# Unused products in the foreseen gaps of TensorE, in a planned convolution and attention kernel

## The chip, the cores and the metric

The kernel runs on one core of a Trainium2 chip. The metric is the device time of one execution in microseconds. TensorE is written PE here, its weight loads PEld, VectorE DVE, ScalarE ACT, GpSimd POOL, and SyncE, which issues most DMAs, SP.

## The reference

The input is 32 images of 128 channels by 64 by 64, in float32, as is everything else. Cut to what matters:

```python
x = x + conv(_gn(x))                  # group norm; 3x3 kernel mixed per image from 4 by a gate
t = _to_tokens(x)                     # 4096 tokens of 128 channels per image
t = t + attn(_ln_t(t))                # 128 -> 16, windows of 144 with stride 72, 4 heads of 4,
                                      # back to 128, added to its input, layer norm
t = t + ffn(_ln_t(t))                 # W, batch norm over all tokens, then a recurrence:
#   y_t = sigmoid(wx_t + y_{t-1} @ V.T)
```

The gate is a softmax over the sigmoid of `pooled @ fc_w.T + fc_b`, with the mean of each channel of the normalised image. The batch norm needs the statistics of all images before the recurrence can start.

## The kernel before, in words

There are two stages. The first, in `images`, runs the convolution, the attention and the product with W for every image and writes the result to `z_d` in DRAM. The second, `by_runs`, is the recurrence; it cuts the 4096 steps into runs of 32 with 16 steps to warm up each and works on four streams at once. The change does not touch it.

In the first stage the work of an image is cut into jobs, each a Python generator that yields before every step and says which engine the step needs and which tiles it reads and writes: `load` (statistics, the gate, the mixed kernel `h`), `taps` and `waves` (the transformed kernels `w` and rows `u` of a fast convolution), `conv` (its products), `drain` (their sum back into `frames`), `project` (layer norm, down to 16 channels), `feed` (queries, keys and values), `values` and `attend` (scores into the tile `sc`, exponentials `ex`, weighted sums into `av`), `divide` (division by the sums, product with `wc` into `sc`, addition to `zt`), `tail` (a layer norm) and `last` (product with `fWc`, statistics). A further job, `setup`, makes constants once.

A planner runs all jobs side by side while the program is built. The class `Clock` keeps for each engine the time at which it is free, and for each tile when it was last written and read, from a table of costs[...]. In each turn the planner takes the job whose next step can start first. Where several can start at the same time, the smaller due time is taken: the image's number plus the first number in `DUE`, plus the second one spread over the job's steps:

```python
a, w, n = DUE.get(job[0], (-1.0, 0.0, 1))
key = at, job[1] + a + w * job[4] / n - (9 if len(job[3]) > 4 else 0)
```

So the order on each engine is the planner's, fixed in the built program[...]. What the planner expects and what the chip does can differ.

[...]`sc` takes four (a single tile for scores and for the divide's products), `nm0` to `nm2` are one bank each and are handed out from the list `nms` to all other products, and one bank is `av`. A step that needs a bank takes it out of `nms` and puts it back once its reader has been recorded. For a step of PE the planner adds 0.25 to the expected start (`SAFE`).

Inside `load`, the gate product is short but stands on a chain: the product `nm<-cv,grp`, then ten small steps of DVE and ACT for the inverse deviation `gr`, then `h<-dev,gr`, then the product with `fcwT`.

In the profile nearly all instructions of the first stage carry one line, L242, since the recording helper issues them; the tiles' names tell them apart. A float32 product appears as two records.

## Time and profile before

| | us |
|---|---|
| median of 3 runs | 4502.47 |
| lowest and highest of them | 4498.48, 4503.09 |
| the profiled execution, own time | 4507.87 |
| its span in the trace | 4506.1 |
| PE busy | 4099.9 |
| DVE busy | 3562.1 |
| ACT busy | 2407.2 |
| POOL busy | 1680.8 |

The mean granted clock of TensorE in the profiled execution is 0.958. The first stage ends near 3962 us, where the recurrence's loads of `z_d` begin; its last 200 us are the drain, in which no new image enters. In a line of the profile's groups, the columns are line, engine, operation, tile written and tiles read, shapes and count, then busy time in us and the mean of one in ns, then the engine's idle time ahead of them and what ended it. In the waits, they are who waited for whom, the total in us, the times and the longest.

### The profile page before, as it was taken

Reading aid. Unit: us, or ns where it says so; the run is one execution under the profiler, and the core shown is the slowest. Engines: PE = TensorE matmul, PEld = TensorE weight load, DVE = VectorE, ACT = ScalarE, POOL = GpSimd, SP = SyncE. Lnnn points to the kernel's source line nnn. Section 1 sums busy time; section 2 is a strip of 40 time slices with the busy share of each in tenths; the row PEclk is TensorE's granted clock in tenths of the full one; section 3 lists DMA queues with packets and bytes.
Section 4 is the critical chain, followed back from the end, with each engine's and each line's share of the span. In section 5 each row is a group of like instructions: output and inputs, shape, how many; then the busy total and the mean of one; then the engine's idle time right before and its main releaser. Section 6 shows DMA issues by size and latency. Waiting matters only on the chain. (4 is left out here: it accounts for less than half of the span.)

```text
span 4506.1 us, 101240 instructions
## 1 busy us (share of the span) xinstructions
PE 4099.9 (91%) x41515; PEld 2055.8 (46%) x41515; DVE 3562.1 (79%) x5364; ACT 2407.2 (53%) x3500; POOL 1680.8 (37%) x1652
## 2 busy tenths in 40 slices
PE   5999889999999999999999999999999997589987
PEld 2444444444444444444444444444444444245443
DVE  7787778888788888788888788888888864459884
ACT  1455545555555555554555555554555565357774
POOL 3443333333334333333334333333333422037665
PEclk9999999999999999999999999999999998789998
DMA  3445454554555555555555456455465544459998
GB/s 101 132 144 161 150 172 153 182 175 157 184 167 177 175 175 182 171 178 166 190 171 180 144 176 189 150 175 177 152 191 166 167 166 168 157 215 257 280 264 170
DMA packets 467567, 789.31 MB, mean 175 GB/s; under 512 B 338048, under 2 KB 348304, under 8 KB 434320
## 3 DMA queue, kind: packets, MB, share of 16 engines
q1 hardware_dynamic: 456480, 715.38, 48.5%
q0 software_dynamic: 8704, 67.11, 7.2%
q8 instruction: 331, 5.42, 0.5%
q14 instruction: 148, 1.21, 0.1%
q10 hardware_dynamic: 1904, 0.18, 0.0%
HBM read 499.06 MB, written 276.76 MB: 172 GB/s over the span
## 5 line engine op out<-in xcount | busy, mean ns | idle before, releaser
L242 ACT ACTIVATE ex<-sc 128x1728 f32<-128x1728 f32 x672 | 1082.5, 1611 | 869.0 <-PE sc L242 854.6
L242 POOL TENSOR_TENSOR qe<-qs,mqk 128x576 f32<-128x576 f32 x448 | 608.8, 1362 | 992.4 <-PE sc L242 990.0
L242 PE MATMUL nm<-u,w 128*128 128x512 f32 x1536 | 779.9, 625 | 24.8 <-POOL w L242 24.6
L242 PE MATMUL sc<-qe,ks 32*128 32x432 f32 (+1 forms) x7168 | 689.0, 455 | 83.9 <-DVE zt L242 39.2
L242 PE MATMUL av<-ex,VE 128*32 128x144 f32 x14336 | 634.2, 296 | 3.0 <-DVE avs L242 2.0
L242 PEld LDWEIGHTS av<-ex,VE 128*32 128x32 f32 x14336 | 396.5, 111 | 309.7 <-issue 250.8
L242 PEld LDWEIGHTS sc<-qe,ks 32*128 32x128 f32 x7168 | 294.0, 190 | 481.7 <-issue 182.2
L1960 PE MATMUL v<-yw,fVT 128*128 128x254 f32 (+1 forms) x1504 | 438.3, 430 | 36.4 <-ACT yw L1973 25.5
L242 POOL TENSOR_TENSOR u<-frames 128x528 f32<-128x528 f32 x256 | 411.1, 1614 | 60.1 <-PE nm L242 57.3
L1971 ACT ACTIVATE yw<-v,shf 128x254 f32<-128x254 f32 (+1 forms) x752 | 353.7, 473 | 123.9 <-DVE v L1966 48.3
L1966 DVE SCALAR_TENSOR_TENSOR v<-zr,scl,v 128x256 f32<-128x256 f32 (+1 forms) x585 | 347.1, 663 | 92.0 <-PE v L1960 91.9
L242 PEld LDWEIGHTS nm<-u,w 128*128 128x128 f32 x1536 | 262.9, 191 | 328.8 <-issue 288.6
L242 PE MATMUL nm<-u,h 128*128 128x512 f32 x768 | 391.1, 622 | 0.5 <-ACT tm L242 0.5
L242 ACT ACTIVATE place<-zt 128x1024 f32<-128x1024 f32 x256 | 261.4, 1052 | 208.1 <-DVE zt L242 180.2
L1960 PEld LDWEIGHTS v<-yw,fVT 128*128 128x128 f32 x1504 | 241.6, 194 | 246.0 <-ACT yw L1971 195.7
L242 POOL TENSOR_TENSOR kt<-ks,mqk 128x384 f32<-128x384 f32 (+1 forms) x96 | 79.4, 827 | 654.8 <-ACT ks L242 432.0
L1977 POOL COPY zr<-yw 128x256 f32<-128x256 f32 x416 | 257.2, 729 | 86.2 <-ACT yw L1971 85.8
L242 PE MATMUL nm<-zt,fWc 128*128 128x512 f32 x512 | 283.5, 649 | 6.3 <-ACT zt L242 6.3
L242 DVE SCALAR_TENSOR_TENSOR u<-u,u 128x528 f32<-128x528 f32 x256 | 247.6, 983 | 25.4 <-POOL u L242 22.8
L242 PE MATMUL nm<-place,avg 128*32 128x256 f32 x3072 | 239.8, 395 | 12.9 <-ACT place L242 12.8
L242 DVE COPY avs<-av 128x288 f32<-128x288 f32 x224 | 100.6, 449 | 190.7 <-PE av L242 189.6
L242 PE MATMUL sc<-avs,wc 17*128 17x288 f32 (+1 forms) x1536 | 174.8, 516 | 69.8 <-DVE zt L242 51.0
(203 smaller groups left out, 6121.3 us busy)
## 6 DMA issues: line engine op xcount, KB each, us to landing
place<-r_d SPq DMA_DIRECT2D x384, 512.0 KB
place<-in_conv_k_dram SPq DMA_DIRECT2D x128, 576.0 KB
x_d<-frames SPq DMA_DIRECT2D x32, 2112.0 KB
place<-x_d SPq DMA_DIRECT2D x128, 528.0 KB
frames<-in_x_dram SPq DMA_DIRECT2D x128, 512.0 KB
out_dram<-zt SPq DMA_DIRECT2D x64, 1024.0 KB
z_d<-zt SPq DMA_DIRECT2D x64, 1024.0 KB
zr<-z_d SPq DMA_DIRECT2D x26, 2048.0 KB
```

The source lines that it names most:

```text
L242: got = f(*args, **kw)
L1960: nc.tensor.matmul(self.ps[:, :, c], fVT, self.yw[1 - r % 2][:, :, c], start=not whole, stop=True)
L1966: nc.vector.scalar_tensor_tensor(v, z, scl, v, ALU.mult, ALU.add)
L1971: nc.scalar.activation(y[:, :, c], self.ps[:, :, c], AF.Sigmoid, bias=shf)
L1977: nc.gpsimd.tensor_copy(z, y)
```

## The change

A constant `SPARE` of three numbers is added, and seven lines in the planner. Whenever the planner has chosen a step of PE, after `setup` is done, it looks at the gap between the time at which PE is free and the step's expected start less 0.3. If that gap is over 0.6 and a bank of `nms` is free by then, it issues products of 128 by 128 by 128 (`fWc` with itself) into that bank until 60% of the gap is filled. Nothing reads them. They are recorded in the planner's `Clock` like any other product. Besides, five entries of `DUE` have other numbers: `setup`, `taps`, `project`, `tail` and `last` are moved and spread differently.

```diff
+SPARE = 0.3, 0.6, 0.6
 DUE = {
-    "setup": (0.27, 0.02, 8),
+    "setup": (0.44, 0.04, 8),
...
-    "taps": (-0.14, 0.29, 6),
+    "taps": (0.04, 0.16, 6),
...
-    "project": (0.55, 0.51, 33),
+    "project": (0.75, 0.37, 33),
...
-    "tail": (2.4, 0.8, 33),
-    "last": (3.05, 0.62, 40),
+    "tail": (2.42, 0.75, 33),
+    "last": (2.99, 0.86, 40),
 }
...
                 job = best[1]
+                if job[3][0] == "PE" and "setup" in done:
+                    at = best[0][0] - SPARE[0]
+                    ready = [t for t in nms if clock.after("PE", t, True) <= clock.free["PE"]]
+                    if ready and at - clock.free["PE"] > SPARE[1]:
+                        t, until = ready[0], clock.free["PE"] + SPARE[2] * (at - clock.free["PE"])
+                        while clock.free["PE"] < until:
+                            nc.tensor.matmul(t[:, 0:P], fWc, fWc, start=True, stop=True)
                 job[4] += 1
                 job[3] = next(job[2], "end")
```

## The prediction

> **What bounds the kernel now.** I read the busy shares and the slices of the page first, then a table of stages, then TensorE's waits, then two of these waits in the timeline.

> ```profile
> PE 4099.9 (91%) x41515; PEld 2055.8 (46%) x41515; DVE 3562.1 (79%) x5364; ACT 2407.2 (53%) x3500; POOL 1680.8 (37%) x1652
> ...
> PE   5999889999999999999999999999999997589987
> ...
> DVE  7787778888788888788888788888888864459884
> ...
> PEclk9999999999999999999999999999999998789998
> ```

> TensorE (PE) is the bound from 112 to 3750 us, VectorE (DVE) stands close behind at eight tenths, and the granted clock is slightly below full nearly everywhere. The stages (columns: PE, PEld, DVE, ACT, POOL busy, clock, DMA share, GB/s):

> ```profile
> 112.00:708.00 596.00, 555.76 (x6170) 275.57 (x6169) 466.98 (x691) 302.91 (x401) 214.20 (x179) 0.97 0.49 154
> ...
> 2126.00:3546.00 1420.00, 1348.12 (x14954) 666.16 (x14953) 1188.72 (x1717) 761.74 (x1020) 504.07 (x409) 0.97 0.54 173
> ...
> 3750.00:3965.00 215.00, 118.26 (x1313) 57.82 (x1306) 102.24 (x156) 80.10 (x104) 20.59 (x16) 0.77 0.45 155
> ```

> Adding up the trace's clock records: from 112 to 3750 us the clock is at half in 36 stretches, 201 us together, and PE is busy for 168.4 us of them. At full clock that work takes half as long, so at most 84 us are lost there. PE is idle for another 195 us of this stage. In the drain (3750 to 3965) 44 us of busy time run at half.

> What opens the gaps, of the waits of PE from 112 to 3750 us (total, times, longest):

> ```profile
> PE sc L242 <- DVE zt L242: 75.5, 39, 4.7
> PE nm L242 <- DVE h L242: 49.7, 19, 3.5
> PE sc L242 <- ACT ex L242: 19.9, 45, 1.2
> ```

> The first wait is the divide's product into the one `sc` tile, which VectorE has not emptied; the second is the gate product with `fcwT` in `load`; the third is the next scores waiting for the exponential. From 708 to 3546 us, 39 gaps of 1.6 us or more hold 106 of 143 us of idle time. The order repeats every three images (355 us), with two late gate products and one pair of divide products in each:

> ```profile
> 1675.17 0.35 PE L242 MATMUL nm<-fcwT,h 128*128 128x4 f32 x2 [2.96 <-DVE h L242]
> ...
> 1694.45 1.01 PE L242 MATMUL sc<-avs,wc 17*128 17x432 f32 x8 [2.49 <-DVE zt L242]
> ...
> 1699.30 0.86 PE L242 MATMUL sc<-qe,ks 32*128 32x144 f32 x8 [3.83 <-DVE zt L242]
> ```

> And the clock around that pair:

> ```profile
> 1693.10:1696.50 3.40, 1.01 (x8) 0.31 (x8) 3.33 (x5) 0.00 (x0) 0.00 (x0) 1.00 0.33 123
> 1696.50:1699.90 3.40, 0.60 (x8) 0.61 (x12) 3.37 (x7) 0.99 (x1) 0.00 (x0) 0.51 0.00 0
> 1699.90:1703.30 3.40, 3.40 (x48) 2.36 (x42) 3.33 (x5) 2.18 (x3) 1.25 (x2) 0.50 0.55 231
> ```

> A stretch with 1.01 us of work is followed by two at half clock. In all 36 cases the 3.4 us ahead hold at most 1.87 us of work.

> [...]

> **The change, part by part.** Compared instruction by instruction, the changed program has 607 unused 128x128 products in 145 groups; 56 groups have two, 30 three, 13 four, 30 five, the last one 72. No other product is added; the DUE values only reorder. The first product of 66 groups waits for the bank's reader (57 ScalarE, 9 VectorE), the others for nothing[...]. From the tenth image on the order again repeats every three images, with 42 unused products in twelve groups, against none.

> *Price of one.* The f32 products nm<-wvB,gt of the same shape are two records 0.112 us apart, so 0.22 us; three took 0.87 us to the next start with the switch, 0.29. I take 0.22: the groups are runs. 607 x 0.22 = 134 us (176 at 0.29), in gaps as far as there are gaps.

> *(a) The clock.* Of the 168.4 us at half, 39.6 follow the divide pair, 70.5 the gate product, 58.3 other waits; half of each is the loss: 20, 35, 29. In the new order no two divide products stand together without 0.86 us of work and five unused products between them: all 20 return. No group stands directly ahead of a gate product, but it is late less often (next part): half, 17.5. Of the others half, 14.5, since the groups stand ahead of products that wait for DVE. **52 us.** Bounds: 0 and 84.

> *(b) The order.* Between the product with cv and the gate product lie VectorE's and ScalarE's steps for gr. PE's own work in between was 3.9, 2.8 and 3.7 us in the three images, and is 2.2, 12.1 and 9.6. In the first of the new ones VectorE's order is like that of before's on-time case, whose chain took 4.1 to 4.2 us: 2.0 us late. In the second, VectorE's work (13 steps, at before's means) is about 12.1: on time. In the third 12.6 against 9.6: up to 3.0 late, I take 1.5. So 3.5 us per cycle, times 10.2 cycles in 3638 us: 36 us instead of 49.7, **14 saved**. The divide pair's 2.49 + 3.83 us (eight times, 50 us) become 2.49 - 0.86 = 1.6 per cycle, 16 us; but the work between scores and the next scores is thinner (0.8 to 1.3 us in seven places, where the next can start 1.73 to 1.82 us after, by before's waits), some 2 us more per cycle, 20 us: **14 saved**. Bounds of (b): 40 lost, 60 gained.

> *(c) Products that outlast their gap.* 18 of the 42 stand ahead of products into sc that can't start before 1.8 us after the last scores: 4.0 us of them in 4.8 us of waiting, but three groups are too long, 0.75 us together. The other 24 fill 60% of what was foreseen, and VectorE was later than foreseen where before shows it; I take a tenth of their 5.3 us. 1.3 us per cycle: **13 us lost**. Bounds: 0 and 134.

> *(d) Given back.* VectorE is busy for 0.83 of the cycle; a faster PE waits for it sooner. A third of (a) and (b): **27 lost**. Bounds: 0 and 60.

> *(e) The drain.* 22 us are lost to the clock there, and 190 unused products stand after the last convolution; PE mostly waits there for VectorE and DMAs, so a third: **7 gained**. Bounds -5 and 22. The recurrence after 3965 us (by_runs) has the same instructions: 0, give or take 5 for where its clock windows fall. The start, with setup and taps later: 0, give or take 8. SP's and POOL's queues get the same DMAs and operations, in another order; their time is in (b).

> Sum: 52 + 14 + 14 - 13 - 27 + 7 = 47 us. The profiled execution took 4507.87 us, so 4461; it stands 5.4 us above the median of the runs, 4502.47: **4455 us**.

> **The rivals.**
> - *Nothing is given back*, and the drain gains fully: 52 + 28 - 13 + 22 = 89, so 4413 us. For it: VectorE still has a sixth of its time free. Against: its waits fall in the same places.
> - *The groups stand where no window was lost.* Only the divide pair's windows return (20), the order brings nothing, 13 are lost to overlong groups and 7 given back: 4502 us, no change. For it: the late gate products get no group of their own. Against: the foreseen waits behind the exponential and the divide are real in before. That an unused product waits itself for its bank and so fills nothing is of this case.
> - *The foreseen gaps are not there* (slower). When PE runs behind the plan, what it waits for is ready, and each group is pure addition, ahead of the product that could start. At 70% of 134 us the loss is 94 instead of 13: 4455 + 81 = 4536 us. It decides from 60 us on, 45% of the products. For it: in before, gaps under 0.9 us hold only 33 us of 2838. Against: the 1.8 us after scores.

> **How the numbers follow.** Forecast 0.63 (4425 to 4490), nothing given back 0.12, no change 0.12, slower 0.13. The range leaves out about one in ten on each side: 4400 to 4522; both ends lie inside the summed bounds above. Faster by over 0.2% (9 us, about what a measurement here can tell): 0.80, with the fast part of the third case; within 0.2%: 0.06; slower: 0.14.

> **What would show it.** Right: half-clock stretches from 112 us to the drain fall from 36 to about 15, with busy time in them from 168 to 65 us; the wait for `h` is 30 to 40 us; nm<-fWc rows of about 1214 records appear, mean clock 0.97 to 0.98. (c) is wrong if sc rows start right at the end of a group where before had none of that wait; (d) if the wait of sc for zt stays under 40 us. The whole is wrong if the half-clock time stays above 160 us, or if PE's idle time falls by less than its busy time grows.

## The result, and the profile after

The changed kernel took 4455.53 us (median of 4 runs, 4448.11 to 4460.42) against 4500.48 us for the kernel before: a ratio of 0.9908, interval 0.9887 to 0.993. Timed again it gave 0.9894 (0.9878 to 0.991). The profiled execution took 4460.42 us and its span is 4458.6 us, against 4507.87 and 4506.1. The forecast was 4455 us.

Parts 1 and 2 of the page of the kernel after, the lines that answer to those of before:

```profile
PE 4180.4 (94%) x42729; PEld 2191.2 (49%) x42729; DVE 3554.4 (80%) x5364; ACT 2410.3 (54%) x3500; POOL 1691.4 (38%) x1652
...
PEclk9999999999999999999999999999999999899998
```

PE has 1214 records more, the 607 products, and is busy for 80 us longer, though the span is 47.5 us shorter. VectorE's work is unchanged. The stages of the kernel after (columns: PE, PEld, DVE, ACT, POOL busy, clock, DMA share, GB/s):

```profile
112.00:1066.00 954.00, 920.04 (x10157) 472.78 (x10156) 776.02 (x1124) 495.19 (x660) 344.80 (x280) 0.98 0.51 161
1066.00:3501.00 2435.00, 2373.78 (x26731) 1222.73 (x26730) 2059.41 (x2996) 1335.03 (x1781) 890.04 (x714) 0.99 0.55 176
...
3705.00:3915.00 210.00, 150.76 (x1592) 93.94 (x1592) 99.62 (x150) 74.56 (x95) 13.76 (x12) 0.84 0.44 153
3915.00:4458.60 543.60, 478.56 (x1620) 265.63 (x1620) 403.14 (x726) 366.66 (x769) 339.17 (x544) 0.94 0.88 239
```

The clock in the middle of the first stage went from 0.97 to 0.99, in the drain from 0.77 to 0.84. The recurrence is as long as it was (544.6 us before, counted from its first product, 543.3 after): all of the gain lies in the first stage. PE's waits after, who waited for whom, total, times, longest:

```profile
PE sc L243 <- DVE zt L243: 33.2, 47, 2.3
...
PE sc L243 <- POOL qe L243: 21.6, 9, 2.9
...
PE sc L243 <- ACT ex L243: 14.4, 54, 0.5
...
PE nm L243 <- DVE h L243: 9.8, 4, 3.8
```

The wait for `zt`, over the whole execution 90.2 us before, fell to 33.2, and the wait of the gate product for `h` from 52.6 to 9.8. New is a wait of the scores for GpSimd's `qe`, 21.6 us in place of 2.6. A wait counts here only from the end of the unused products that stand in it, so a smaller one need not mean that its product came earlier.

For a balance I cut the stretch from 112 us to the recurrence's first product into four terms. *Clock* is half of the time that PE is busy while the clock records say half: in before, the records of the product `nm<-u,w` (128x512) start 854 ns apart at half clock and 429 ns at full (medians of 13 and 1074 intervals). In before and after the clock records say 1 or 0.5 and, but for the last one of each, have lengths in multiples of 3.413 us; such a stretch is what the forecast calls a window. *Unused* is the number of unused products in the stretch times 0.22 us (at full clock their records, two to a product, start 112 ns apart in the kernel after). *Idle* is the time without a PE record. *Work* is what is left. All four are worked out from the one profiled execution of each kernel, in us; sums in the text are taken before rounding. The names other than before and changed are the experiments of the next section.

| kernel | stretch | work | unused | idle | clock |
|---|---|---|---|---|---|
| before | 3849.5 | 3454 | 0 | 291 | 105 |
| changed | 3803.3 | 3460 | 129 | 164 | 50 |
| change_again | 3807.5 | 3462 | 129 | 168 | 47 |
| planned_only | 3823.9 | 3444 | 0 | 298 | 82 |
| doubled | 3853.0 | 3446 | 259 | 117 | 31 |
| large_groups | 3807.7 | 3448 | 85 | 227 | 48 |
| small_groups | 3810.7 | 3457 | 44 | 244 | 65 |
| untold | 3842.9 | 3474 | 126 | 184 | 59 |
| gate_fill | 3840.4 | 3459 | 24 | 276 | 82 |
| measured_fill | 3815.3 | 3466 | 43 | 247 | 59 |
| queries_fill | 3803.1 | 3466 | 140 | 169 | 28 |
| due_only | 3909.0 | 3443 | 0 | 349 | 117 |
| spare_only | 3905.2 | 3463 | 148 | 222 | 73 |

From before to changed, idle and unused together stay the same (291 and 294 us): the gaps are as long as they were, and the unused products lie in them. What is gone is 55 us of half clock; work rose by 6. The balance compares single executions: between before and planned_only the stretch differs by 26 us, but the medians on one chip by 16, so differences of some 10 us in it are no finding.

### The profile page after: what moved, and what is told of

The parts are those of the page before. It is cut to its first block, busy times and chain, and to the rows that moved or that the text cites. A ratio compares the mean times of both kernels' runs of the same rounds, so it can differ in the third digit from the quotient of the medians.

```text
span 4458.6 us, 103741 instructions
## 1 busy us (share of the span) xinstructions
PE 4180.4 (94%) x42729; PEld 2191.2 (49%) x42729; DVE 3554.4 (80%) x5364; ACT 2410.3 (54%) x3500; POOL 1691.4 (38%) x1652
## 4 chain that ended last, share of the span: by engine, by line
PE 61%; DVE 20%; DMA 9%; issue 4%; ACT 2%; SPq 2%; POOL 1%; DVEq 0%; ACTq 0%; POOLq 0%
PE nm L243 33%; PE sc L243 13%; PE av L243 10%; DVE zt L243 6%; PE v L1968 3%; DVE v L1974 3%; DVE frames L243 2%; DMA zr<-z_d 2%; DVE cp L243 2%; SPq L243 2%; ACT ex L243 2%; DMA out_dram<-zr 2%; DVE h L243 1%; DVE st L243 1%; DMA place<-x_d 1%
## 5 line engine op out<-in xcount | busy, mean ns | idle before, releaser
L243 PE MATMUL sc<-qe,ks 32*128 32x432 f32 (+1 forms) x7168 | 669.6, 443 | 41.9 <-POOL qe L243 21.6
L243 PE MATMUL av<-ex,VE 128*32 128x144 f32 x14336 | 624.6, 292 | 5.7 <-DVE avs L243 5.4
L243 POOL TENSOR_TENSOR u<-frames 128x528 f32<-128x528 f32 x256 | 392.8, 1544 | 37.1 <-PE nm L243 34.5
L243 ACT ACTIVATE place<-zt 128x1024 f32<-128x1024 f32 x256 | 259.8, 1050 | 175.9 <-DVE zt L243 166.6
L243 DVE SCALAR_TENSOR_TENSOR zt<-sc,gbk,zt 128x576 f32<-128x576 f32 (+1 forms) x192 | 174.5, 909 | 70.0 <-PE sc L243 69.0
L243 DVE TENSOR_TENSOR zt<-frames,place 128x1024 f32<-128x1024 f32 x128 | 211.5, 1682 | 21.2 <-DMA place<-r_d 21.2
L243 ACT COPY zt<-nm 128x512 f32<-128x512 f32 x256 | 149.1, 584 | 141.0 <-PE nm L243 139.7
```

Source lines behind the costliest of these rows:

```text
L243: got = f(*args, **kw)
```

## The experiments

My theory was that the clock brings the gain, and that the order counts only in how it lays out the gaps. The rivals were that the new order saves waiting, and that VectorE takes back what a faster PE gains. All ratios are to the kernel before, run on the same chip as the kernel in question.

**The changed order without the products.** They are noted in the planner's clock, so that every engine has the changed order, and not issued:

```diff
-                            nc.tensor.matmul(t[:, 0:P], fWc, fWc, start=True, stop=True)
+                            clock.note("PE", "matmul", (t[:, 0:P], fWc, fWc), dict())
```

> The changed order on every engine, but the 607 unused products are only noted in the planner's clock and not issued. Theory (the products keep the clock, the order brings little): the half-clock stretches come back, PE busy in them from 100 to about 190 us between 112 us and the recurrence, so some 45 us lost: 4495 to 4505 us, like before. Rival (the new order brings the gain by its shorter waits, the products cost about what they bring): 4455 to 4475 us.

Measured: 4482.51 us, ratio 0.997 (0.9957 to 0.9982). Between the two expectations: the order alone brings 0.3%, the products on top of it some 0.7% (0.9908 and 0.9894 against 0.997). The balance suggests how the order does it: not by less waiting (298 us idle against 291), but by less half clock, 82 us against 105, and 10 us less work. The waits of PE in this run:

```profile
PE sc L243 <- DVE zt L243: 76.0, 50, 4.1
PE sc L243 <- ACT ex L243: 41.4, 75, 1.8
...
PE nm L243 <- DVE frames L243: 29.0, 25, 1.9
...
PE nm L243 <- DVE h L243: 9.8, 4, 3.8
```

With the order alone all but four of the gate product's late arrivals are gone; in their place there are more and shorter waits, for the exponential (28.2 us in before) and for `frames` (8.1 us in before). From 112 us to the drain 28 half-clock stretches are left of 36. That the shorter gaps are the reason is inferred from this; no run tests it by itself.

**The same products with one column.** After the notes, as many products as were noted are issued, with the same bank and the same waits, but one column:

```diff
+                        for _ in range(n):
+                            clock.nc.tensor.matmul(t[:, 0:1], fWc, fWc[:, 0:1], start=True, stop=True)
```

> The changed order, and every unused product is issued with one column instead of 128, with the same bank and the same waits. Theory[...]: as without the products, 4495 to 4507 us, with half-clock time as there. Rival (the early wait for the bank's reader, or merely something issued in the gap, brings the gain): 4455 to 4470 us.

Measured: 4489.95 us, ratio 0.9982 (0.9972 to 0.9992), and a mean clock of 0.961 against 0.963 without any product and 0.975 with the full ones. The group of these products and that of the full ones (columns: line, engine, operation, tiles, shapes and count; busy us, mean ns of one; idle ahead). With one column:

```profile
L1423 PE MATMUL nm<-fWc 128*128 128x1 f32 x1214 | 188.4, 277 | 0.8 <-DVE frames L243 0.8
```

In the kernel after, with 128:

```profile
L243 PE MATMUL nm<-fWc 128*128 128x128 f32 x1214 | 175.9, 291 | 0.4 <-DVE frames L243 0.4
```

In the profile both fill PE for about the same time, and both come with 1214 weight loads. Only with the full ones was the mean clock higher than without any product, 0.975 against 0.963. Of the other products, 150 us run at half clock here, 164 in planned_only and 88 in the changed kernel. So something merely issued in the gap, or an earlier wait for the bank, does not bring the gain. The one-column products are no gain over none at all (4489.95 us against 4482.51, with intervals that overlap).

**Before's order with products that the planner isn't told of.**

```diff
+                        f = clock.free["PE"]
+                        while f < until:
+                            clock.nc.tensor.matmul(t[:, 0:P], fWc, fWc, start=True, stop=True)
+                            f += 0.22
```

> The kernel before with its own due numbers and its own order; 592 unused products fill 60% of the gaps that its plan foresees, and the planner is not told of them. Theory (clock): the pair of divide products no longer lets the clock fall, the late gate products still do, as no plan foresees them; about 20 to 35 of the 84 us return and 10 are lost to overlong groups: 4475 to 4490 us. Rival (the order is what counts): no change, 4495 to 4510 us. Rival (products alone bring all): 4455 us.

Measured: 4503.74 us, ratio 1.0014 (1.0005 to 1.0023), slower than before by a hair and in the range of the rival that expected no change, though not for its reason: the clock's mean rose to 0.974, and its loss fell from 105 to 59 us. I had expected 10 us of cost; the balance shows 39: idle and unused together went from 291 to 310, and work rose by 20. So here a higher clock brought no time by itself. The gate product stayed late:

```profile
PE nm L245 <- DVE h L245: 53.1, 20, 3.4
```

**Twice as many products**, `range(2 * n)` with full columns.

> The changed order, with two unused products for each one of the change (1214, nominally 120% of the foreseen gaps). Theory (the gaps are real and mostly as long as foreseen or longer): a group outlasts its gap by some 20 to 40% of the gap's 0.22 us steps, so of the 134 us added 40 to 70 lie on the path, while the clock returns 5 to 10 us more: 4485 to 4520 us. Rival (the chip runs later than planned, the gaps have room): 4445 to 4465 us. Rival (the gaps are hardly there): over 4560 us.

Measured: 4510.34 us, ratio 1.003 (1.002 to 1.004). Of the 129 us added in the stretch, idle time took up 47, the clock returned 19 more, to a loss of 31, and work fell by 14; the other 50 us made the stretch longer: that unused products hold up the work behind them was the forecast's assumption, and here it is the nearest reading. The forecast range held. The gaps have some room left at 60% but not at 120%; nothing in between was run.

**Large groups only, small groups only**: `n if n > 3 else 0` (405 products in 59 groups), and `n if n <= 3 else 0` (202 in 86).

> The changed order; of the unused products only the 405 that stand in the 59 groups of four or more are issued, the 202 in groups of two or three are only noted. Theory (long gaps let the clock fall, short ones don't, and a short gap is filled or overrun at no use): the clock stays as with all groups, PE busy at half 95 to 115 us against 99, and the small groups' cost of up to 10 us goes: 4445 to 4460 us. Rival (all gaps count alike, so two thirds of the products bring two thirds of the gain between 4482 without products and 4455): 4464 us. Rival (the short ones alone hold windows just above the limit): 4470 us or more.

> The changed order; only the 202 products in the 86 groups of two or three are issued. Theory (long gaps count): the half-clock time stays that of the order without products, 150 to 170 us of busy time, and the small groups cost up to 10 us: 4480 to 4495 us. Rival (all count alike): 4473 us. Rival (the short ones count): 4455 to 4462 us.

Measured: 0.9901 (0.9883 to 0.9918) with the large ones, at 4462.66 us against 4505.16, and 0.9941 (0.9925 to 0.9958) with the small ones, at 4476.53 us. The large groups alone give what the change gives; the clock's loss is 48 us there and 50 with all groups. The saving of 10 us that I expected from dropping the small ones can't be seen: work is 12 us lower, but idle and unused together are 18 higher. The small ones alone stand 0.3% under the order without products (0.997), against my theory that short gaps count for nothing; 0.9941 is what the rival expected that counts all alike (4473 us of 4500). But the two intervals just touch, and the ratios come from two chips, so this is weakly shown. With both, the small ones add nothing that can be seen.

**Each half of the change with its own plan**: the new due numbers without SPARE, and SPARE with the old numbers.

> The five new due numbers without SPARE; the planner makes another order, in which the cycle of three images doesn't appear. Theory (the due numbers fit the plan with products in it and have no worth of their own): no faster than before, 4495 to 4540 us, as the order jumps between patterns. Rival (the due numbers bring the 0.3% that the changed order brought by itself): 4475 to 4490 us.

> SPARE and its seven lines with the due numbers of before; 693 products in 162 groups, told to the planner, which makes another order without a cycle of three images. Theory (the products keep the clock in any order, but overrun their gaps where the order is not in step): clock 0.97 or more, half-clock busy time 100 to 120 us, time 4480 to 4510 us. Rival (the products alone, told to the planner, bring the gain): 4450 to 4465 us.

Measured: due_only 4566.31 us, ratio 1.013 (1.011 to 1.0149); spare_only 4561.29 us, ratio 1.0123 (1.0105 to 1.0141). Both are slower than either expectation. The clock loss is 117 us in the first and 73 in the second; what costs the time is the gaps, 349 us idle in one and 370 idle and unused in the other against 291. Neither order falls into the cycle of three images. So neither half of the change is a gain by itself; the numbers suit the plan that has the products in it, and the 0.3% of planned_only belong to that plan.

**Products at the late gate product, in before's order.** Here the gap is known from the trace, not from the plan; `unused(t, n)` issues n of the products into bank t, and the planner isn't told:

```diff
+                if b >= 5 and b % 3 != 1:
+                    unused(lg_ps, 6)
                 nc.tensor.matmul(lg_ps[:, 0:NK], pl, fcwT, start=True, stop=True)
```

> The kernel before, its order and plan unchanged; six unused products (108 in all) stand directly ahead of each of the 18 gate products that came 2.2 to 3.0 us late in its trace. Theory (a stretch of 3.4 us with under 1.9 us of work costs the clock, and at an unchanged order half or more of the clock's gain reaches the end): PE busy at half falls by some 55 us, 27 us at full clock, of which VectorE lets half through: 4480 to 4490 us against 4500. Rival (VectorE's chain sets the pace there, a faster PE only waits longer): idle time grows by what the clock returns, 4495 to 4505 us. Rival (all comes back): 4473 us.

Measured: 4495.93 us, ratio 0.9966 (0.9953 to 0.9978). One of these places in its timeline (start, duration, what, idle time ahead):

```profile
1659.13 1.50 PE L461 MATMUL nm<-fWc 128*128 128x128 f32 x12
1661.69 0.39 PE L242 MATMUL nm<-fcwT,h 128*128 128x4 f32 x2 [1.05 <-DVE h L242]
```

The clock in stretches of 3.4 us around such a place in before, where the product came at 1675.17 us:

```profile
1672.70:1676.10 3.40, 0.93 (x8) 0.96 (x8) 3.02 (x9) 0.20 (x2) 1.99 (x2) 0.99 0.37 142
1676.10:1679.50 3.40, 3.40 (x34) 1.52 (x33) 1.22 (x5) 1.72 (x4) 0.00 (x0) 0.50 0.23 68
```

and around the place above:

```profile
1659.30:1662.70 3.40, 2.35 (x20) 2.11 (x19) 3.03 (x9) 0.65 (x2) 1.99 (x2) 1.00 0.62 184
1662.70:1666.10 3.40, 3.20 (x54) 2.06 (x56) 2.53 (x9) 2.70 (x8) 0.00 (x0) 1.00 0.15 44
```

The stretch with the wait now has 2.35 us of work in place of 0.93, the product comes when VectorE is ready, and the clock stays full. Of the 18 places, 16 had a half-clock stretch within 4 us in before, and one has here. That shows the cause of these stretches. The clock's loss fell by 23 us, less than the 27 expected, since new half-clock stretches came up elsewhere; 15 us (0.34% of 4509) reached the end. As a share of before, which took 4509.53 us on this chip, that lies in the range of the theory. The wait for `zt` grew:

```profile
PE sc L242 <- DVE zt L242: 99.8, 47, 4.7
```

It was 90.2 us in before, so some of the gain was given back in waiting for VectorE.

**Also at the divide pair**, 196 products in all.

```diff
+                        pair = d and b % 3 == 0 and 6 <= b < 30
+                        if pair and u and nms:
+                            unused(min(nms, key=lambda t: clock.after("PE", t, True)), 5)
...
+                        if pair and u and nms:
+                            unused(min(nms, key=lambda t: clock.after("PE", t, True)), 6)
```

> As gate_fill, and also five unused products ahead of the second divide product of the pair, and six after it, in the eight images where the trace of before had waits of 2.5 and 3.8 us there (196 products in all). Theory (clock, half reaches the end): 20 us more of the clock's loss return, 4467 to 4482 us, near the changed kernel, which would show that gaps measured on the chip serve as well as gaps foreseen. Rival (the wait is VectorE's own time and ends when it ends): as gate_fill within 5 us.

Measured: 4491.02 us, ratio 0.996 (0.9944 to 0.9975), as gate_fill within 5 us, as the rival said. But 0.996 is also the edge of the theory's range taken as a share (4482 us of 4500), so this run doesn't decide between them. The clock's mean rose from 0.963 to 0.969, as means over all executions, with little to show for it in the time. One of the six executions took 4473 us and the others 4487 to 4496; the profile and its row of the balance are of that one, so I don't read the gap between the two kernels from it.

**Products at GpSimd's wait, in the changed kernel**, six at each of eight places.

```diff
+                        if i == 2 and m == 3 and b >= 8 and b % 3 == 2 and nms:
+                            unused(min(nms, key=lambda t: clock.after("PE", t, True)), 6)
```

> The changed kernel with 48 more unused products, six at each of the eight places where its trace still shows PE waiting some 2.5 us for GpSimd's qe in a mixed scores step, which no plan foresaw; the planner is not told. Theory: these eight half-clock stretches of 3.4 to 6.8 us go, 15 us of loss return, half or more of it reaches the end: 4440 to 4450 us against 4455. Rival (GpSimd sets the pace there): no change, 4452 to 4460 us.

Measured: 4470.97 us, ratio 0.9913 (0.9897 to 0.993), no better than the change. The half-clock stretches there are gone, the clock's mean is 0.980 and its loss 28 us in place of 50. But idle and unused together are 308 in place of 294, and work 3466 in place of 3460: what the clock returned was taken back in full. The profile is of the shortest of five executions. The time did not change, as the rival expected; that GpSimd sets the pace there, its reason, is not shown.

**The change once more**, as the measure for the last ones.

> The changed kernel itself once more, with more rounds, as the measure for the kernels that come close to it. Theory (its gain is 0.9%, and neither the large groups alone nor the products at GpSimd's wait improve on it): ratio 0.989 to 0.993 to before, overlapping 0.9901 of the large groups and 0.9913 of the added products. Rival (its first ratio was a fast sample): 0.994 or more, and the large groups alone would be the better version.

Measured: 4461.61 us, ratio 0.9894 (0.9878 to 0.991). No kernel tried is shown to be faster than the change, and large_groups is not shown to be slower.

## Why the prediction was right, point by point

- *The bound* was read rightly: PE in the first stage. What the change won there is half clock, 55 us, and not waiting.
- *(a), the clock, 52 us.* Measured from 112 us to the drain: busy time at half went from 168.4 to 66.7 us, 51 us at full clock. The size was right. planned_only still has 116.2 us there, so 26 us came with the order and 25 with the products; the forecast had 17.5 from the order, 14.5 from the products and 20, at the divide pair, from both. The mark of 65 us was met, and that of 15 stretches too.
- *(b), the order, 28 us.* Wrong. The order without the products is not idle for less than before's (298 against 291 us). The gate product, put at 36 us, was better than I said, and missed the mark of 30 to 40 us: 9.8 us of waiting, all of it before 860 us. In the changed order's cycle it is never late:

```profile
1640.49 0.28 PE L243 MATMUL nm<-cv,grp 128*128 128x1 f32 x2
...
1643.33 0.28 PE L243 MATMUL nm<-fcwT,h 128*128 128x4 f32 x2
```

  Its chain ended 2.2 us after the product with cv, where I took 4.2 from before's on-time case; there VectorE reached its first step 2.4 us after that product, here 0.4, and from there on the chain (seven small steps up to `gr`, not ten) took 1.8 us in both. In the other two images the chain ended after 13.1 and 12.9 us and PE arrived after 14.1 and 13.0; I had put PE at 12.1 and 9.6. But the wait for `zt`, where I put 34 us saved, fell by 14 in planned_only (from 90.2 to 76.0), and the small waits that I put at 20 us more were 54 (13 more for the exponential, 21 for `frames`, 20 for `qe`).
- *(c), overlong groups, 13 us.* Not there as described. Between planned_only and the change, idle time fell by 134 us, as much as the 129 of unused products: taken together, the groups did not outlast their gaps. Work rose by 16 us, a loss of about the size forecast. It is not a higher price of the products: with twice as many, in doubled, work is only 2 us over planned_only. Its cause is open.
- *(d), given back, 27 us.* Not there between planned_only and the change, where idle and unused together went from 298 to 294. The wait of sc for zt was 33.2 us, under the 40 named as the mark against it, but the unused products stand in that wait, so the mark says less than the sum. Elsewhere part of the clock's return was lost: about a third in gate_fill, as forecast here, and all of it in queries_fill. Why not in the change is open.
- *(e), the drain, 7 us.* It went from 212 to 210 us, so 2 us gained. The recurrence is 1.3 us shorter, within its bounds; the start can't be read apart, since the stretch is cut at 112 us in both.

So (b) and (d), 28 and 27 us, were both absent and cancelled; without both the sum is 52 - 13 + 7 = 46. That the forecast came out to the microsecond is luck; that the clock is the term that counts is not. Of the rivals, "the groups stand where no window was lost" has the outcome of untold, but not its reason, as 46 us of clock came back there; "the foreseen gaps are not there" comes nearest in doubled, where 50 of the 129 us added lengthened the stretch. The idea that products alone, in any order, bring the gain fell with untold and spare_only.

What stays open: why queries_fill and untold give back nearly all that their clock returns while the change gives back little, why the small groups seem to bring 0.3% alone and nothing that can be seen beside the large ones, and what the work term holds, which rose by 16 us from planned_only to the change and by 20 from before to untold.

## What to carry to other kernels

Where TensorE is near its bound and the clock records show half-rate stretches, count the busy time in them: half of it is what can be won at most where, as here, the same product takes twice as long at half clock (854 against 429 ns from record to record). Here it was 105 us, more than any single wait. How much of it reaches the end has to be measured: in untold none did. Look for single long gaps before many short ones (0.9901 with the large groups alone, 0.9941 with the small ones), and try first to lay the gaps out more evenly or to fill the long ones in part. Here 60% paid, and at 120% the products cost more than the clock returned. A planner's constants and what the planner is told belong together: each half of this change alone made the kernel 1.2 to 1.3% slower.

## What the runs showed of the hardware that I had not expected

Products of one column filled PE in the profile for as long as full ones (188.4 against 175.9 us) and came with as many weight loads (1214), yet the mean clock was 0.961, against 0.963 without any product and 0.975 with the full ones. The stretches themselves show it. One of them and the 3.4 us ahead of it, with the columns of the table of stages:

```profile
856.70:860.10 3.40, 3.40 (x33) 2.67 (x29) 2.80 (x5) 0.59 (x1) 0.00 (x0) 1.00 0.62 193
860.10:863.50 3.40, 3.40 (x17) 2.11 (x17) 3.33 (x5) 0.00 (x0) 0.00 (x0) 0.50 0.04 4
```

PE shows as busy for the whole of the first stretch, and half clock follows. From 112 us to the recurrence, 16 of the 30 half-clock stretches of this run follow 3.4 us in which PE shows 2.35 us of work or more; without the one-column products none of the 30 has over 2.06 us. So neither a PE that shows as busy nor the weight loads kept the clock here, while with as many products of 128 columns its mean was higher (0.975). What in them makes the difference is not shown: only these two widths were run.
